# Two decoder layers on one core: which engine copies layer 0's results out of PSUM

## The chip, the cores and the metric

The kernel runs on one core of a Trainium2 chip. The time is the device time of one execution in microseconds (us). A core has five engines with a queue each, which work in parallel and meet through semaphores: PE (TensorE, the matmuls, with its weight loads PEld), DVE (VectorE), ACT (ScalarE), POOL (GpSimd) and SP, which here only issues DMAs. Matmul results land in PSUM, and an engine has to copy them from there to SBUF before a later matmul can read them.

## The reference, cut to what matters

The input x is 4 x 256 x 512 in fp32. Two layers follow each other, each an attention and a linear layer with residuals and layer norms. In layer 0 the attention has 32 heads of 16 channels, in 8 groups of keys and values, with a causal mask:

```python
q = (x @ Wq + bq).reshape(B, S, NUM_HEADS, HEAD_DIM).transpose(0, 2, 1, 3)
k = (x @ Wk + bk)...   # 8 kv heads, each repeated for 4 query heads
scores = jnp.einsum('bhqd,bhkd->bhqk', q, k) / jnp.sqrt(HEAD_DIM)
scores = jnp.where(causal, scores, NEG)
p = jax.nn.softmax(scores, axis=-1)
out = jnp.einsum('bhqk,bhkd->bqhd', p, v).reshape(B, S, D_MODEL) @ Wo + bo
x = _layernorm(x + out)
x = _layernorm(x + x @ W.T + bias)      # W dequantised from q_vals, q_scales
```

Layer 1 does the same with 32 heads of 128 channels, biases by distance, and another linear layer. The change doesn't touch it.

## The kernel before, in words

Layer 0 runs in 64 steps, one for each (b, qt, e, i): four sequences b; two tiles qt of 128 query tokens; and two times four groups e, i of four heads. A step with qt = 0 sees 128 keys, one with qt = 1 sees 256, so that eight steps of 128 keys and eight of 256 take turns. `begin0` (L477) makes a step's scores: four matmuls with 32 rows each (L486) into `sc`, which is four PSUM banks and has one buffer only (`ps_s0`). DVE adds the causal mask while it moves them to SBUF (L489) and takes the negated maximum of each row (L495); ACT makes the exponentials, one instruction for each of four heads with the sum as a second output (L278); DVE inverts the sums (L283) and POOL multiplies by them (L286).

`run` (L327) sets the order. Iteration n calls `before0` for step n, then `begin0` for step n; then `fill` advances the work that fills PE's gaps; then `transpose0` is called for step n-4, and `end0` for step n-6. `transpose0` transposes the probabilities on PE, one PSUM bank with four 128 x 128 blocks for each 128 keys (L301), and has the bank copied to `prT` by `evacuate`: one copy for a step of 128 keys, two for one of 256. After eight steps `end0` has multiplied `prT` with the values (L534) into `o`, which is copied to `oT`, and starts `tail0` for that tile of tokens: output projection py (L442), norm, transpose to `x1T`, linear layer pf (L459), norm, transpose to `x2T` for layer 1. The work that `fill` advances is these tails, the dequantisation and transposition of the linear layer's weight (L206), and `project0` (L372), the q, k and v of the next sequence. The transposes and all these projections share one pool of three PSUM banks, `ps_w`.

Since transposes lag by four steps, the iterations that begin steps of 256 keys copy for four steps of 128 keys and four of 256, and so do those that begin steps of 128. The engine queues in the compiled kernel are not in the order of the code: the framework orders instructions when it compiles, by dependencies and estimated costs of its own, except where the code asks for program order.

`evacuate` (L98) is the one place where the engine of these copies is chosen. It is called for `prT` (L302), for the transposed x, x1 and x2 (L275), for the weight's transposes (L225) and for `oT` (L543). It counts calls, and gives a copy to DVE (L103) or ACT (L105):

```python
if turn[0] % shares[0] == 1 and not last:
    nc.vector.tensor_copy(dst, src)
else:
    nc.scalar.copy(dst, src)
```

In layer 0 `shares[0]` is 3, so that each third copy is DVE's. At L576, after layer 0's loop, it becomes 2, and layer 1 alternates. Layer 1 begins with PE filled by the projections p_k, p_q and p_v (L636), while the last tails of layer 0 end beside it.

Of the kernel before, what the change touches and what calls it, by code (L numbers as in the profile page):

```python
# [61 lines left out]
def block_kernel(  # L62
# [29 lines left out]
    dram = pool(ctx, "dram", 4, space=bass.MemoryType.DRAM)  # L92

    turn = [0]
    shares = [3]
    last = []

    def evacuate(dst, src):  # L98

        if not last:  # L100
            turn[0] += 1
        if turn[0] % shares[0] == 1 and not last:
            nc.vector.tensor_copy(dst, src)  # L103
        else:
            nc.scalar.copy(dst, src)  # L105
# [100 lines left out]
    def feed_forward_weight():  # L206

        for _ in range(G):
            yield True
        nb = D // BLK  # L210
        for oc in range(NC):
            ins = nc.vector.scalar_tensor_tensor(
                wf_n[:, oc, :].rearrange("p (n k) -> p n k", k=BLK),
                qv[:, oc, :].rearrange("p (n k) -> p n k", k=BLK),
                -128.0,
                qs[:, oc, :].unsqueeze(2).to_broadcast([P, nb, BLK]),
                ALU.add,
                ALU.mult,
            )
            tc.keep_in_program_order(ins)  # L220
            yield True
            pw = bank_t(f"pw_{oc}")
            for ic in range(NC):
                nc.tensor.transpose(pw[:, ic, :], wf_n[:, oc, ts(ic, P)], ident)
            evacuate(wfT[:, :, ts(oc, P)], pw)  # L225
        yield True
# [10 lines left out]
    def load_weights1(kv):  # L237
        wq1 = w1.tile([P, NC, G * P], F32, tag="wq1", name=f"wq1_{kv}", bufs=1)
        wo1 = w1.tile([P, G, D], F32, tag="wo1", name=f"wo1_{kv}")
        if kv % 2 == 0:  # L240
            wk1 = w1.tile([P, NC, 2 * P], F32, tag="wk1", name=f"wk1_{kv}", bufs=1)
            nc.sync.dma_start(wk1, w_qkv_v[:, :, NQ + kv * P : NQ + (kv + 2) * P])
            wk_pair[kv // 2] = wk1
        nc.sync.dma_start(wq1, w_qkv_v[:, :, ts(kv, G * P)])
        weights1[kv] = (wq1, wo1)
        if kv == 0:
            load_output_weight(kv)
# [22 lines left out]
    def transposed(dst, src, name):  # L270

        pt = bank_t(f"pt_{name}")
        for c in range(NC):
            nc.tensor.transpose(pt[:, c, :], src[:, ts(c, P)], ident)
        evacuate(dst, pt)  # L275
# [20 lines left out]
    def transposed_probabilities(name, pr, parts):  # L296

        for kt, dst in parts:
            pt = bank_t(f"pt_{name}_{kt}")
            for i in range(G):  # L300
                nc.tensor.transpose(pt[:, i, :], pr[:, i, ts(kt, P)], ident)  # L301
            evacuate(dst, pt.rearrange("p i (j q) -> p i j q", q=32))  # L302
# [43 lines left out]
    def advance(queue):  # L346

        while queue:
            if next(queue[0], None) is not None:
                return  # L350
            queue.popleft()

    def exhaust(queue):
        while queue:
            advance(queue)
# [189 lines left out]

    def before0(step):
        b, qt, e, i = step
        if (qt, e, i) == (0, 0, 0):
            if b == 0:
                for _ in range(3):  # L550
                    advance(ahead)
            else:
                exhaust(ahead)
            if b + 1 < B:
                ahead.append(project0(b + 1))
            if b == 1:
                load_weights1(0)

    def fill():
# [8 lines left out]
        transpose0,  # L568
        end0,
        before0,  # L570
        fill,
        lag=4,
        more=2,
        rest=divide0,
    )
    shares[0] = 2  # L576
    la.close()


# [527 lines left out]
```

## Time and profile before

| what | us |
|---|---|
| median of three runs | 951.85 |
| the three runs | 948.67, 951.85, 1353.63 |
| profiled execution, its own time | 951.23 |
| its span, from first to last instruction | 949.3 |
| PE busy in the span | 906.8 (96%) |
| DVE busy | 623.8 (66%) |
| ACT busy | 333.9 (35%) |
| POOL busy | 444.7 (47%) |

The profile is of one execution. Busy times are of an engine's instructions, a matmul's end is modelled, so that a busy PE is not a PE at its peak. Rows of groups give: line, engine, operation, output and input by the program's names, shapes and count; busy time and mean ns of one; idle time just before them and what ended it. Rows of the timeline give start, length, engine, line and operation, and in brackets the idle time before and what ended it. Layer 0 takes about the first 260 us; its steps of 256 keys begin at 38.5, 98.1, 160.4 and 217.2 us.

### The profile page before, as it was taken

The page shows a single profiled execution, that of the slowest core. Times are in us where ns is not written, and L with a number is a line of the kernel's source. Part 1 is how long each engine was busy: PE and PEld are TensorE (multiplying, and loading weights), DVE is VectorE, ACT ScalarE, POOL GpSimd, SP SyncE. Part 2 cuts the span into 40 slices and gives each one's busy share as a digit, 9 for nine tenths or more (in the row PEclk, how much of TensorE's full clock was granted, in tenths as well). Part 3 has the DMA queues.
Part 4 walks back from the last instruction along what each step waited for, and adds up shares of the span by engine and source line. Part 5 has one row for each costly group of instructions (what it writes and reads, how often), then busy time and mean ns, then how long its engine had stood idle before and what let it go on. Part 6 is the DMA issues. An engine that isn't in the chain of part 4 may idle for free.

```text
span 949.3 us, 11860 instructions
## 1 busy us (share of the span) xinstructions
PE 906.8 (96%) x3849; PEld 554.4 (58%) x3849; DVE 623.8 (66%) x1269; ACT 333.9 (35%) x1216; POOL 444.7 (47%) x462
## 2 busy tenths in 40 slices
PE   7998999898899999999999999999999999999996
PEld 5755555554444445666666566666666666667652
DVE  3986978879434448555676776666666666666566
ACT  2775675677410003323222222122221121214441
POOL 2554553645356124426434533643553534656732
PEclk9999999999999999999999999999999999999998
DMA  9500000000020103543443443353353333432001
GB/s 246 185 1 1 1 2 1 1 1 1 1 89 22 45 1 89 152 111 115 114 130 79 134 132 100 110 140 88 117 139 95 122 89 105 129 89 70 1 34 55
DMA packets 76419, 74.46 MB, mean 78 GB/s; under 512 B 5957, under 2 KB 52678, under 8 KB 76358
## 3 DMA queue, kind: packets, MB, share of 16 engines
q1 hardware_dynamic: 75014, 72.02, 26.4%
q10 hardware_dynamic: 1344, 1.70, 0.6%
q8 instruction: 30, 0.49, 0.2%
q14 instruction: 31, 0.25, 0.1%
HBM read 49.58 MB, written 24.12 MB: 78 GB/s over the span
## 4 chain that ended last, share of the span: by engine, by line
PE 70%; DVE 12%; POOL 9%; ACT 5%; DMA 2%; issue 1%; ACTq 0%; POOLq 0%; SPq 0%; DVEq 0%
PE p_q L636 19%; PE po L885 14%; PE sc L972 7%; PE o L1012 7%; PE p_k L636 5%; PE p_v L636 5%; ACT pr L278 4%; PE py L442 3%; DVE pr L489 3%; PE pf L459 2%; DVE nm L495 2%; PE py L846 2%; POOL x L907 2%; POOL pr L286 2%; DVE prT L103 1%
## 5 line engine op out<-in xcount | busy, mean ns | idle before, releaser
L286 POOL TENSOR_TENSOR pr<-pr,sums 128x512 f32<-128x512 f32 (+1 forms) x128 | 189.5, 1481 | 232.9 <-DVE sums L283 227.4
L278 ACT ACTIVATE pr<-sc,nm 128x128 f32<-128x128 f32 (+1 forms) x256 | 105.0, 419 | 291.1 <-DVE nm L988 277.1
L278 ACT ACTIVATE pr<-pr,nm 128x128 f32<-128x128 f32 (+1 forms) x256 | 113.2, 444 | 39.3 <-DVE sums L283 30.2
L980 DVE SCALAR_TENSOR_TENSOR sc<-table,sc 128x128 f32<-128x128 f32 (+1 forms) x256 | 86.0, 356 | 34.7 <-PE sc L972 32.4
L972 PEld LDWEIGHTS sc<-kT,qT 128*128 128x128 f32 x512 | 82.3, 191 | 35.1 <-issue 29.7
L972 PE MATMUL sc<-kT,qT 128*128 128x256 f32 (+1 forms) x512 | 95.0, 327 | 0.0
L1012 PE MATMUL o<-prT,v 128*128 128x512 f32 x192 | 92.9, 592 | 0.0
L312 DVE STREAM_TRANSPOSE blocks<-pr 128x512 f32<-128x512 f32 x84 | 57.6, 698 | 45.2 <-POOL pr L286 45.1
L650 DVE TENSOR_TENSOR qT<-p_q,qT 128x512 f32<-128x512 f32 x96 | 64.6, 686 | 33.6 <-PE p_q L636 32.8
L988 DVE TENSOR_REDUCE nm<-sc 128x2 f32<-128x512 f32 (+1 forms) x128 | 70.0, 550 | 1.5
L489 DVE TENSOR_TENSOR pr<-sc,causal 128x512 f32<-128x512 f32 (+1 forms) x64 | 60.5, 945 | 10.2 <-PE sc L486 10.0
L301 PE MATMUL pt<-ident,pr 128*128 128x128 f32 x432 | 59.9, 276 | 7.2 <-DVE prT L103 2.1
L495 DVE TENSOR_REDUCE nm<-pr 128x4 f32<-128x512 f32 (+1 forms) x64 | 60.7, 948 | 1.2
L301 PEld LDWEIGHTS pt<-ident,pr 128*128 128x128 f32 x432 | 48.6, 141 | 21.2 <-issue 10.1
L105 ACT COPY o<-o 128x512 f32<-128x512 f32 x29 | 17.0, 587 | 124.9 <-PE o L1012 124.9
L885 PE MATMUL po<-wo,so 128*128 128x256 f32 x224 | 58.0, 381 | 2.1 <-POOL so L616 2.1
L636 PE MATMUL p_q<-x2T,ws_q 128*128 128x512 f32 x128 | 59.8, 592 | 0.0
L636 PE MATMUL p_q<-xt,ws_q 128*128 128x512 f32 x128 | 57.7, 592 | 0.0
L885 PE MATMUL po<-wo,o 128*128 128x256 f32 x224 | 57.7, 380 | 0.0
L636 PE MATMUL p_q<-x2T,wq 128*128 128x512 f32 x128 | 57.6, 592 | 0.0
L105 ACT COPY prT<-pt 128x512 f32<-128x512 f32 x76 | 42.6, 582 | 39.5 <-PE pt L301 39.5
L885 PE MATMUL po<-to,so 128*128 128x256 f32 x224 | 53.3, 381 | 1.0 <-POOL so L619 1.0
(159 smaller groups left out, 1516.8 us busy)
## 6 DMA issues: line engine op xcount, KB each, us to landing
way<-blocks SPq DMA_DIRECT2D x112, 128.0 KB, 2.5
prT<-way SPq DMA_DIRECT2D x28, 512.0 KB, 3.7
wq<-in_L_attn_w_qkv_dram SPq DMA_DIRECT2D x8, 1024.0 KB, 5.1
wo<-in_L_attn_w_o_dram SPq DMA_DIRECT2D x8, 1024.0 KB, 5.4
way<-blocks SPq DMA_DIRECT2D x112, 64.0 KB, 1.8
prT<-way SPq DMA_DIRECT2D x28, 256.0 KB, 2.6
wk<-in_L_attn_w_qkv_dram SPq DMA_DIRECT2D x4, 512.0 KB, 3.8
wv<-in_L_attn_w_qkv_dram SPq DMA_DIRECT2D x2, 1024.0 KB, 6.2
```

The costliest lines, as they stand in the source:

```text
L278: nc.scalar.activation(pr[:, i, 0:w], sc, AF.Exp, bias=nm[:, i : i + 1], accum_out=sums[:, i : i + 1])
L286: nc.gpsimd.tensor_tensor(pr[:, :, 0:w], pr[:, :, 0:w], sums.unsqueeze(2).to_broadcast([P, G, w]), ALU.mult)
L301: nc.tensor.transpose(pt[:, i, :], pr[:, i, ts(kt, P)], ident)
L489: nc.vector.tensor_tensor(pr[:, :, 0:w], sc[:, :, 0:w], causal[:, 2 * P - w :].unsqueeze(1).to_broadcast([P, G, w]), ALU.add,)
L495: nc.vector.tensor_reduce(nm, pr[:, :, 0:w], AX.X, ALU.max, negate=True)
L636: nc.tensor.matmul(bank, fixed, moving, start=(c == 0), stop=(c == 1))
L650: add = lambda dst, a, b: nc.vector.tensor_tensor(dst, a, b, ALU.add)
L885: nc.tensor.matmul(bank[:, ts(n, HALF)], left[:, c, :], right[:, c, :], start=(c == 0), stop=(c == 1),)
L972: nc.tensor.matmul(sc[:, m, 0:w], qT[:, 2 * j + m, b * S + qt * P : b * S + (qt + 1) * P], kT[:, b * S : b * S + w], start=True, stop=True,)
L980: nc.vector.scalar_tensor_tensor(sc[:, m, 0:w], table[:, 2 * P - w :], slopes[kv * G + 2 * j + m], sc[:, m, 0:w], ALU.mult, ALU.add,)
L988: nc.vector.tensor_reduce(nm[:, 2 * j : 2 * j + 2], sc[:, :, 0:w], AX.X, ALU.max, negate=True)
L1012: nc.tensor.matmul(o, v1[:, 2 * b + kt, ts(kv, P)], prT[:, kt].rearrange("p j h q -> p h j q"), start=(kt == 0), stop=(kt == qt),)
```

## The change

The share is now a pattern which the counter walks through, and it depends on the kind of the step that begins in this iteration. With 128 keys (qt = 0) two of three copies go to DVE; with 256 keys (qt = 1) none does. After the last step the pattern of 256 keys stays in force until the loop of layer 0 has ended, and layer 1 has the pattern (0, 1).

```diff
-    shares = [3]
+    shares = [(1, 1, 0)]
...
-        if turn[0] % shares[0] == 1 and not last:
+        if shares[0][turn[0] % len(shares[0])] and not last:
             nc.vector.tensor_copy(dst, src)
         else:
             nc.scalar.copy(dst, src)
...
     def before0(step):
         b, qt, e, i = step
+
+        shares[0] = ((1, 1, 0), (0,))[qt]
         if (qt, e, i) == (0, 0, 0):
...
-    shares[0] = 2
+    shares[0] = (0, 1)
```

## The prediction, made before the changed kernel had run

> **What bounds the kernel now.** I read the page first, for where TensorE (PE) is short of work:
>
> ```profile
> PE   7998999898899999999999999999999999999996
> ...
> DVE  3986978879434448555676776666666666666566
> ACT  2775675677410003323222222122221121214441
> ```
>
> Each digit is a fortieth of the span, 23.7 us. From the twelfth slice (260 us) on PE is full: layer 1 waits for matmuls and nothing else, so a microsecond won or lost in layer 0 arrives at the end whole, and only layer 0 is at stake. Next I cut layer 0 into the stretches in which it begins steps of 256 keys (first, third, fifth and seventh line) and of 128 keys, by the start times of the mask additions of L489. The columns are us, then busy time of PE, weight loads, DVE (VectorE), ACT (ScalarE), POOL, then the granted clock:
>
> ```profile
> 38.50:67.60 29.10, 26.92 (x187) 16.83 (x186) 25.61 (x39) 21.70 (x71) 15.39 (x11) 0.94 0.01 1
> 67.60:98.10 30.50, 28.08 (x188) 16.92 (x187) 20.41 (x44) 18.73 (x79) 13.62 (x13) 1.00 0.00 1
> 98.10:130.20 32.10, 28.85 (x195) 17.71 (x196) 28.97 (x44) 20.87 (x71) 17.42 (x13) 1.00 0.01 2
> 130.20:160.40 30.20, 29.16 (x192) 17.17 (x191) 21.10 (x46) 19.36 (x80) 13.78 (x13) 1.00 0.00 1
> 160.40:192.30 31.90, 29.02 (x195) 17.67 (x195) 29.07 (x44) 21.13 (x72) 17.29 (x13) 1.00 0.00 1
> 192.30:217.20 24.90, 22.44 (x168) 12.35 (x167) 18.53 (x40) 18.51 (x77) 12.49 (x12) 1.00 0.00 1
> 217.20:244.00 26.80, 22.47 (x144) 11.45 (x144) 24.59 (x38) 21.22 (x74) 15.90 (x11) 1.00 0.00 1
> ```
>
> In the 256-key stretches DVE is busy 108.2 of 119.9 us (90%), ACT 84.9 (71%); in the three 128-key ones DVE 60.0 of 85.6 (70%), ACT 56.6 (66%). Yet PE is above 83% everywhere, so this is no plain DVE bound. What PE waits for from 24 to 260 us, with total, times and longest:
>
> ```profile
> PE sc L486 <- DVE pr L489: 8.6, 13, 1.5
> PE py L442 <- ACT oT L105: 3.3, 6, 0.7
> PE pt L301 <- DVE prT L103: 2.1, 2, 1.1
> PE pt L301 <- ACT prT L105: 1.9, 4, 0.7
> ```
>
> All PE waits of that window, with another 1.2 for an oT copied on DVE and small ones, come to 21.6 us: the ceiling of any gain by this change, 2.3%. The largest is the scores' single set of banks, which DVE's mask addition must empty before the next step.
>
> **The change, part by part.** Followed through the code, the counter of `evacuate` reaches 132 in both versions. Before, 44 copies go to DVE: 20 of 59 in iterations that begin a 256-key step, 20 of 60 in 128-key ones, 3 of 10 after the last step, 1 of 3 in layer 1. After, it is 0 of 59, 39 of 60, 0 of 10, 1 of 3. Layer 1 alternates on the same parity as before, so nothing changes there. Prices:
>
> ```profile
> L105 ACT COPY prT<-pt 128x512 f32<-128x512 f32 x64 | 35.9, 579 | 33.8 <-PE pt L301 33.8
> L103 DVE COPY prT<-pt 128x512 f32<-128x512 f32 x32 | 21.7, 678 | 1.3 <-PE pt L301 1.3
> ```
>
> The Trainium skill, "ScalarE: Activation LUTs", section "Rules for kernel authors", puts simple elementwise work (add, mul) on VectorE and not on ScalarE. If a copy counted as such, moving 20 of them to ACT would be a loss; by the rows it is a gain of 0.1 us of engine time each, 2.0 us for 20, given back by the 19 that go the other way. I take the rows: these copies read PSUM in fp32. So no work disappears; it changes place.
>
> *256-key stretches.* DVE loses 20 x 0.678 = 13.6 us, to 94.6 of 119.9 (79%); ACT gains 20 x 0.579 = 11.6, to 96.5 (80%). Averages do not price this; the bursts do, in which PE has little other work. In them a step costs DVE 1.21 + 1.21 + 0.17 = 2.6 us (addition, maximum, reciprocal), and ACT 2.08 (four exponentials in the chain) plus, in the second half of the stretch, two copies, 1.15: 3.2. Before, with a third of two copies on DVE, it was 3.05 against 2.85. So the burst goes from DVE-bound to ACT-bound at much the same rate. Replayed on the timeline, the third stretch of the table above:
>
> ```profile
> 117.07 0.51 ACT L278 ACTIVATE pr<-pr,nm 128x256 f32<-128x256 f32 x1 [2.30 <-DVE sums L283]
> ...
> 119.43 0.66 DVE L103 COPY oT<-o 128x512 f32<-128x512 f32 x1
> ...
> 120.14 3.70 PE L442 MATMUL py<-wop,oT 128*128 128x512 f32 x8 [1.20 <-DVE oT L103]
> ```
>
> Without the DVE copy of prT at 115.18 (0.67 us), the maximum, the exponentials and the next addition come 0.6 earlier. The moved copy fits in ACT's 2.30 us pause. The exponentials end at 118.55, then prT and oT in turn on ACT, 119.7, so py starts at 119.7 in place of 120.14: -0.5. At 48 to 56 us ACT has no such pause (idle 0.3 before each group of exponentials): two moved copies push oT and py from 55.87 to about 56.5, +0.6. At 175 to 182 the 0.6 won on DVE is spent on a third copy in a row on ACT: 0. At 228 to 236: two more copies against a 0.95 pause, +0.2. Together +0.3. Bounds: all waits ended by DVE in these stretches vanish (6.05 by the addition, 2.2 by copies): -8.3; or each of the 20 stands behind a group of exponentials and costs PE the 0.7 of the longest ACT waits: +14. The replay is nearest to the rows and is taken.
>
> *128-key stretches.* 16 of the 19 copies are in the three stretches: DVE +10.8, to 70.9 of 85.6 (83%), ACT -9.3, to 55%. Gains: x1T of tile 0 and oT of tile 1 leave the ACT queue, where PE waited 0.43 (73.9 us) and 0.73 (88.4) for them: -1.2. Loss: five waits for the addition (2.6 us in all) can each have a copy of 0.6 put in front; half of that, +1.5. Bounds -2.6 and +6. Taken +0.3. The cover is the runs of projections (py and pf last 3.7 us each), in which DVE works off what it owes; without it all 10.8 would show.
>
> *The first 128-key stretch*, 24.0 to 38.5, has DVE at 13.04 of 14.5. Three more copies (2.0 us) make 15.1, over the stretch: +0.6 (bounds 0 and 2.0). The one in front of the dequantisation delays PE's pw transposes, already waiting 1.35 there.
>
> *After the last step* the transposes at 244.68 waited 1.10 for a DVE copy that stood behind an addition; on ACT it follows two copies at 243.4: -0.6. At 253.4 two copies ran on both engines at once; on ACT in a row: +0.6. Sum 0. No DMA, buffer or queue of SP or POOL moves.
>
> *The clock.* One stretch ran throttled:
>
> ```profile
> 52.00:56.00 4.00, 2.25 (x23) 0.61 (x19) 3.96 (x7) 3.63 (x13) 2.49 (x3) 1.00 0.00 0
> 56.00:60.00 4.00, 4.00 (x6) 1.71 (x7) 2.12 (x3) 3.63 (x15) 3.44 (x2) 0.58 0.02 4
> ```
>
> After 4 us at 56% busy the clock fell to 0.58, and a py of 3.7 us took 5.4, 1.7 us lost. The Trainium skill, "TensorE: Matmul & The Clock Gate", section "What's actually happening", has the clock fall after an idle window of about 3.4 us. By that rule nothing here is near it (PE's longest wait is 1.55) and the sum gets no term; by the row a thin burst is enough, and the term is -1.7 if the change thickens this burst, +1.7 for another that thins. By my replay this burst gets no denser: 0, and 1.7 to the range.
>
> Sum: 0.3 + 0.3 + 0.6 + 0 + 0 = +1.2. The profiled execution took 951.23 (span 949.3), the median of three is 951.85; 951.85 + 1.2 = **953.0 us**.
>
> **The rivals.** *It cancels* (chance 0.52): 953, own range 948 to 958. *DVE was the bound* (0.22): for it speak its 90% and the 8.6 us; against, that ACT is needed by the same steps and rises to 80%. Most of the 8.3 goes, the first stretch takes some back: -6, 946, down to 940; over 2% needs nearly all 21.6 us of waits to go. *The copies stand behind exponentials on ACT* (0.21), the other clear sign: ACT runs in order, a group blocks 2.08 us, and three banks serve transposes and projections alike. For it speak the 3.3 us for oT and 1.9 for prT; against, that the 39 copies already on ACT there cost PE 0.1 us each. At that 0.1 the move costs 2.0 and is covered; it decides from about 0.4 us per moved copy: 20 x 0.5 = +10, 962, with a tail to 975. *The order itself shifts* (0.05): queues are not in code order (a copy stands between an addition and its maximum at 99.25), so another order may be found, either sign, 3 us.
>
> A measurement of this kernel can tell about 2%, 19 us, from no change. Faster by that is the edge of the second case, 0.03; slower the tail of the third, 0.08; within, 0.89. Range: 944 leaves out the lower part of the second case, 962 the upper half of the third.
>
> **What would show it.** 44 copies on DVE become 40, none in 256-key stretches after 40 us; DVE there near 79%, ACT near 80%; waits of PE for DVE's addition fall there, those for ACT's prT and oT rise by about as much; 24 to 38.5 grows by under a microsecond; from p_k (260.4 us) on the same length as before. The sum fails if PE waits for ACT in the 256-key stretches by far more or less than for DVE before, or if layer 1 changes length.

## The result, and the profile after

The changed kernel took 943.61 us (median of seven runs, 942.18 to 946.05) against 951.85 before; the ratio is 0.9934, with a 95% interval of 0.9917 to 0.9952, so -6.3 us (-7.9 to -4.6) on 950. In a second comparison, further down, it was 0.9927 (0.9910 to 0.9944). The first execution of before, 1353.63, was a disturbed one and is left out of every comparison. The forecast was 953, the range 944 to 962. The median lies 0.4 us below the range: the change is worth 0.7%, within 2%, but it goes the other way, and its -6 is the size of the second rival, 946. Some 2 us of the distance to 953 are the base: the forecast stood on 951.85, and in the later comparisons the medians of before were 949.1 to 949.9.

The rows of the page of the changed kernel, in fortieths of a span of 942.5 us:

```profile
PE   7989899898999999999999999999999999999996
...
DVE  3987978888324457655766676667675766666566
ACT  2785765768410014232222222221221122214441
```

PE is full from the eleventh slice on, as it was from the twelfth. Layer 1's first p_k starts at 253.7 us in place of 260.4, and from there to the end it takes 688.8 us, before 688.9. All of the gain is in layer 0, and all of it arrives.

The same stretches as before, cut at the starts of L489's additions, with the columns us, then busy time of PE, weight loads, DVE, ACT, POOL, and the granted clock:

```profile
39.20:66.70 27.50, 24.87 (x183) 15.76 (x182) 23.30 (x34) 23.68 (x77) 15.81 (x11) 1.00 0.01 1
66.70:95.70 29.00, 28.23 (x193) 17.06 (x191) 23.50 (x50) 16.94 (x74) 13.60 (x13) 1.00 0.00 1
95.70:126.40 30.70, 28.31 (x191) 17.24 (x192) 26.60 (x40) 22.81 (x75) 17.45 (x13) 1.00 0.01 2
126.40:156.20 29.80, 28.80 (x197) 17.51 (x195) 23.66 (x50) 16.19 (x72) 13.17 (x13) 1.00 0.00 1
156.20:187.70 31.50, 28.39 (x191) 17.25 (x192) 26.59 (x39) 23.80 (x79) 17.92 (x13) 1.00 0.01 1
187.70:211.80 24.10, 22.64 (x180) 12.63 (x177) 20.27 (x45) 16.87 (x72) 12.75 (x12) 1.00 0.00 1
211.80:236.00 24.20, 19.90 (x137) 10.56 (x130) 21.35 (x32) 21.62 (x77) 15.93 (x11) 1.00 0.00 1
```

The last line ends where the last addition of layer 0 starts. In the prediction's table the last line ends at 244.0, where that addition ends. Cut at its start, the line of before is:

```profile
217.20:242.70 25.50, 21.74 (x140) 11.03 (x140) 23.29 (x36) 20.48 (x73) 15.90 (x11) 1.00 0.00 1
```

So before had 118.6 us in the 256-key stretches, with DVE at 106.9 (90%) and ACT at 84.2 (71%). Now DVE is at 97.8 of 113.9 us (86%) and ACT at 91.9 (81%); in the 128-key stretches DVE is at 67.4 of 82.9 (81%) and ACT at 50.0 (60%). Every stretch of the table is shorter: those of 256 keys by 4.7 us together, of which 1.7 is the clock (below), and those of 128 keys by 2.7. The stretch ahead of the table is 0.4 longer.

What PE waited for, from 24 to 260 us:

```profile
PE sc L486 <- DVE pr L489: 6.1, 14, 1.0
PE py L442 <- ACT oT L105: 6.0, 7, 1.4
PE pt L301 <- ACT prT L105: 2.4, 3, 1.0
PE o L534 <- ACT prT L105: 1.4, 2, 0.7
```

The wait for the mask addition fell by 2.5 us and the wait for oT rose by 2.7, much as forecast. All waits of PE add up to 19.2 us, before 21.6. That is 2.4 of a gain of 6.7 between the two profiles. The weight loads (PEld) waited for the same addition too, and longer; first before, then after:

```profile
PEld sc L486 <- DVE pr L489: 22.1, 26, 2.5
```

```profile
PEld sc L486 <- DVE pr L489: 18.5, 24, 1.7
```

The rest of the gain is in time that the profile calls busy for PE. These are the sums over layer 0, from 17 us to the first p_k, of before and then of after:

```profile
sum 243.40, PE 221.42 PEld 133.17 DVE 192.52 ACT 162.04 POOL 122.45; mean PE 24.60 PEld 14.80 DVE 21.39 ACT 18.00 POOL 13.61
```

```profile
sum 236.70, PE 217.38 PEld 132.21 DVE 190.33 ACT 163.43 POOL 122.80; mean PE 24.15 PEld 14.69 DVE 21.15 ACT 18.16 POOL 13.64
```

PE did the same matmuls in 4.0 us less of "busy". About 1.7 of it is the clock (below); for the rest the groups of PE tell, the values' product o for one, first before, then after:

```profile
L534 PE MATMUL o<-prT,v 128*32 128x512 f32 x192 | 31.2, 601 | 1.0 <-ACT prT L105 0.9
```

```profile
L534 PE MATMUL o<-prT,v 128*32 128x512 f32 x192 | 29.1, 601 | 1.4 <-ACT prT L105 1.4
```

The mean of one is the same 601 ns, their union is 2.1 us shorter: they lie closer together. The Trainium skill, "Trainium Kernel Development and Optimization", section "Performance Expectations", warns that matmul busy time is a bad measure of how close a kernel is to the roofline, since matmuls are pipelined; in this pair of rows it falls by 2.1 us for 192 matmuls of an unchanged mean.

### The profile page after: what moved, and what is told of

Same layout as the page of the kernel before. It is cut to its first block, busy times and chain, and to the rows that moved or that the text cites. A ratio compares the mean times of both kernels' runs of the same rounds, so it can differ in the third digit from the quotient of the medians.

```text
span 942.5 us, 11859 instructions
## 1 busy us (share of the span) xinstructions
PE 902.2 (96%) x3849; PEld 552.9 (59%) x3849; DVE 621.4 (66%) x1265; ACT 335.7 (36%) x1220; POOL 445.0 (47%) x462
## 4 chain that ended last, share of the span: by engine, by line
PE 73%; DVE 10%; POOL 9%; ACT 4%; DMA 2%; issue 1%; ACTq 0%; SPq 0%; POOLq 0%; DVEq 0%
PE p_q L638 19%; PE po L887 14%; PE sc L974 7%; PE o L1014 7%; PE p_k L638 5%; PE p_v L638 5%; PE py L442 3%; ACT pr L278 3%; PE pf L459 3%; DVE pr L489 2%; DVE nm L495 2%; PE py L848 2%; POOL x L909 2%; PE pt L301 2%; POOL pr L286 2%; PE sc L486 1%
## 5 line engine op out<-in xcount | busy, mean ns | idle before, releaser
L489 DVE TENSOR_TENSOR pr<-sc,causal 128x512 f32<-128x512 f32 (+1 forms) x64 | 60.6, 947 | 7.8 <-PE sc L486 7.1
L301 PEld LDWEIGHTS pt<-ident,pr 128*128 128x128 f32 x432 | 48.7, 141 | 19.2 <-issue 8.0
L105 ACT COPY prT<-pt 128x512 f32<-128x512 f32 x82 | 44.7, 586 | 27.4 <-PE pt L301 27.3
```

What stands on the lines that cost most here:

```text
L489: nc.vector.tensor_tensor(pr[:, :, 0:w], sc[:, :, 0:w], causal[:, 2 * P - w :].unsqueeze(1).to_broadcast([P, G, w]), ALU.add,)
```

## The experiments

All ran with timing against the kernel before on the same chip. The differences are ratios times 950 us, with their intervals. The clock is the mean over a kernel's runs of the granted clock; before had 0.9950 to 0.9955. A clock lower by 0.001 is 0.1%, about 1 us here; half_b, below, shows a fall that comes at least in part of the kernel itself, so such a difference is not always chance.

| kernel | 256-key steps, DVE | 128-key steps, DVE | us against before | clock |
|---|---|---|---|---|
| the change | none | 2 of 3 | -6.3 (-7.9 to -4.6) | 0.9957 |
| after_again | none | 2 of 3 | -6.9 (-8.6 to -5.3) | 0.9960 |
| only256 | none | 1 of 3 | -4.2 (-5.2 to -3.0) | 0.9957 |
| only128 | 1 of 3 | 2 of 3 | -0.7 (-2.1 to +0.8) | 0.9942 |
| third2 | another third | another third | -1.6 (-2.9 to -0.4) | 0.9949 |
| third0 | another third | another third | -1.5 (-3.2 to +0.1) | 0.9949 |
| allact | none | none | +7.9 (+5.7 to +10.0) | 0.9907 |
| full128 | none | all | -0.5 (-1.9 to +1.0) | 0.9943 |
| half_a | none in the first four | 1 of 3 | -2.6 (-3.8 to -1.2) | 0.9955 |
| half_b | none in the last four | 1 of 3 | +1.4 (+0.1 to +2.8) | 0.9931 |
| dve_load | none, and spare additions | 2 of 3 | +8.4 (+5.9 to +10.8) | 0.9913 |
| dve_load2 | none, and 23 reductions | 2 of 3 | +0.8 (-0.7 to +2.1) | 0.9943 |
| act_load | 1 of 3, and 23 ACT copies | 1 of 3 | +2.6 (+1.4 to +3.7) | 0.9945 |
| dve_a | none, and 8 reductions | 2 of 3 | -1.0 (-2.6 to +0.4) | 0.9936 |
| dve_b | none, and 15 reductions | 2 of 3 | -4.5 (-5.8 to -3.2) | 0.9966 |
| ot_dve | none but oT | 2 of 3 and oT | -7.1 (-9.5 to -4.7) | 0.9966 |
| best | none but oT | 1 of 3 at first, then 2 of 3; oT | -9.8 (-11.8 to -7.9) | 0.9968 |

**The two halves of the change, and all on ACT.** The patterns are edited where the change set them:

```diff
# only256
-    shares = [(1, 1, 0)]
+    shares = [(0, 1, 0)]
-        shares[0] = ((1, 1, 0), (0,))[qt]
+        shares[0] = ((0, 1, 0), (0,))[qt]
# only128
-        shares[0] = ((1, 1, 0), (0,))[qt]
+        shares[0] = ((1, 1, 0), (0, 1, 0))[qt]
# allact
-    shares = [(1, 1, 0)]
+    shares = [(0,)]
-        shares[0] = ((1, 1, 0), (0,))[qt]
+        shares[0] = ((0,), (0,))[qt]
```

> Half of the change: steps of 256 keys all on ACT, steps of 128 keys as before (one of three on DVE). Theory A (DVE set the pace in the 256-key stretches, relief there is the gain): all of it or more, -6 to -8 us against before. Theory B (the recorded one: DVE's relief and ACT's load cancel there): 0 to +1. Theory C (scatter: any other choice of which third of the copies goes to DVE moves the time by several us): no rule, between -6 and +6.

> The other half: steps of 128 keys two of three on DVE, steps of 256 keys as before. Theory A: +1 to +3 us against before, DVE gets 19 more copies and nothing in return. Theory B: +1. If the gain of the whole change lies in the 128-key stretches, because ACT is relieved there, -3 to -5.

> All copies of layer 0 on ACT, in steps of 128 keys too: DVE is relieved in both stretches, ACT takes 43 copies more. Theory A: in the 256-key stretches as good as the change; in the 128-key ones ACT rises from 66% to about 80%, DVE falls to 58%, so -5 to -9 us against before if only DVE counts, and worse than the change if the two of three on DVE matter there. Theory B: 0 to +5.

only256 won 4.2 us, two thirds of the whole; by the prediction's account it had to be 0 to +1. only128 is not to be told from before, at a lower mean clock (0.9942 against 0.9953, 1.0 us of the span); the rest of the change beside only256 is 2.1 us. allact lost 7.9, so it was not DVE alone that counted: in the 128-key steps a third of the copies on DVE is worth 12 us. There the exponentials and all copies stand in one queue, and where PE is short of work the clock is low too. Four stretches of 4 us in the profile of allact, with the columns as above:

```profile
72.00:76.00 4.00, 3.21 (x15) 2.37 (x14) 1.46 (x3) 2.92 (x11) 1.36 (x2) 0.50 0.00 0
76.00:80.00 4.00, 4.00 (x12) 2.40 (x11) 0.00 (x0) 2.71 (x10) 0.60 (x1) 0.66 0.01 4
212.00:216.00 4.00, 2.06 (x14) 1.09 (x15) 2.04 (x5) 3.39 (x16) 2.08 (x2) 0.91 0.00 0
216.00:220.00 4.00, 4.00 (x7) 1.53 (x6) 0.00 (x0) 0.28 (x2) 0.00 (x0) 0.67 0.00 0
```

At 0.50 to 0.91 the clock costs about 5 us in these 16; the stretches themselves are 34.5 and 31.7 us long, before 30.5 and 24.9.

**All on DVE in 128-key steps.**

```diff
# full128
-    shares = [(1, 1, 0)]
+    shares = [(1,)]
-        shares[0] = ((1, 1, 0), (0,))[qt]
+        shares[0] = ((1,), (0,))[qt]
```

> Steps of 256 keys all on ACT, steps of 128 keys all on DVE. All-ACT in the 128-key steps cost 12 us against one in three on DVE, and two of three won another 1 to 2. If DVE at two of three is near its limit (83% in the table): +2 to +6 against the changed kernel. If ACT's relief still counts: -1 to -3 against the changed kernel, -7 to -9 against before.

The 256-key steps stay on ACT; DVE's share of the copies in 128-key steps is none, one, two or three of three in allact, only256, the change and full128: +7.9, -4.2, -6.3, -0.5. Two of three is near the best of these, and both ends cost. The first 128-key stretch of full128 took 23.7 us, before 21.7, in the change 22.1: there DVE has the weight's dequantisation as well. The four 128-key stretches of full128 are 6.1 us longer than those of the change.

**Scatter: another third.** Two kernels give DVE one copy in three everywhere, as before, but others.

```diff
# third2
-    shares = [(1, 1, 0)]
+    shares = [(0, 0, 1)]
-        shares[0] = ((1, 1, 0), (0,))[qt]
+        shares[0] = ((0, 0, 1), (0, 0, 1))[qt]
# third0: the same with (1, 0, 0)
```

> One copy of three on DVE in all steps, as before, but the next third of them (43 DVE copies in layer 0 in place of 43, other ones). Theories A and B: within 1.5 us of before. Theory C: it moves by 4 us or more, either way, and the result of the change is no proof of a mechanism.

> A second other choice of one copy in three for DVE in all steps (43 in layer 0, as before; five oT and two x1T among them). Scatter of the choice alone: within 2 us of before if the load counts, 4 us or more either way if the choice does.

Both came out about 1.5 us below before, third2 clear of zero and third0 just not. So the choice of copies, at the same load, can move the time by that much; a gain of 6 is more than this scatter, the 0.7 of only128 is not.

**What a load costs.** The first attempt added unused additions on DVE; `extra` is a flag that is on in 256-key steps and at the end:

```diff
# dve_load, on the change
+            if extra and turn[0] % 3 == 1:
+                nc.vector.tensor_tensor(spare, fb_b, fb_b, ALU.add)
```

> The changed kernel, with an idle DVE addition of 128x512 in SBUF (0.69 us) traced at each place in the 256-key steps and at the end where the copy was DVE's before: 23 of them, which nobody waits for. DVE has its old load back, ACT keeps the copies. Theory A (DVE's load was the cost): the 256-key gain of about 4 us is lost, so -1 to -3 against before. If only the place of the copies mattered, not the load: -5 to -7, as the changed kernel. If ACT's load were the gain's limit: no change either.

It went to +8.4 and says less than it seems. The timeline shows all 23 additions between 36.5 and 89 us, and some of them 1.2 to 2.3 us long beside POOL: they depend on nothing, and the ordering at compile time pulled them forward. The next two tie the spare work to its place by its input:

```diff
# dve_load2, on the change; out is a slice of spare in the shape that is needed
+        if extra and turn[0] % 3 == 1:
...
+            nc.vector.tensor_reduce(out, dst, AX.X, ALU.max)
# act_load, on the kernel before, in the same places
+        if extra and turn[0] % 3 == 1:
...
+            nc.scalar.copy(out, dst)
```

> The changed kernel, with a reduction on DVE of each tile that a moved copy has just written (128x512, about 0.68 us, result unused), at the 23 places in 256-key steps and at the end where the copy was DVE's before. Unlike the spare additions of the earlier run it can't run ahead of its place. DVE has its old load back there, ACT keeps the copies. If DVE's load was what the 256-key half won, the time goes back by 4 us or more: -2 to +4 against before. If DVE has slack there, it stays within 1.5 us of the changed kernel: -5 to -7.

> The kernel before, with a second copy on ACT of each tile that DVE copied in a 256-key step or at the end (SBUF to SBUF, about 0.6 us, unused). ACT has the changed kernel's load there, DVE keeps its own. If the prediction's ACT bound is real (ACT 80% busy costs about what DVE's relief gains): +4 or more against before. If ACT has slack in those stretches: within 1.5 us of before.

Against the changed kernel (ratio 0.993 in the mean of its two comparisons) dve_load2 lost 7.4 us: 23 reductions of 0.66 us cost 0.32 each. act_load lost 2.6 against before: 23 copies of 0.62 us cost 0.11 each. 7.4 less 2.6 is 4.8, about the 4.2 that only256 won. In its wait list the price of dve_load2 is seen at once (the added code moves these lines down by 9):

```profile
PE sc L495 <- DVE pr L498: 12.5, 12, 2.9
PE py L451 <- ACT oT L106: 3.1, 6, 0.7
```

The wait for the mask addition doubled from the 6.1 of the changed kernel. In act_load it stayed about as it was before (8.3, before 8.6), and what rose is the wait for oT:

```profile
PE sc L495 <- DVE pr L498: 8.3, 13, 1.2
PE py L451 <- ACT oT L106: 4.5, 6, 1.1
```

Each spare instruction also waits for the copy that it reads (1.2 and 1.1 us in two waits on DVE, 6.0 us in six on ACT), so both prices are upper ones. And the price of dve_load2 is not spread evenly: 3.8 of the 7.3 us between its profile and that of the change lie in the last stretch, where one DVE instruction took 2.11 us in place of 0.55. The next runs show the same thing.

**Where DVE's load bites.** First by halves of the 256-key relief:

```diff
# half_a (half_b: (1, 1)), on the change
-    shares = [(1, 1, 0)]
+    shares = [(0, 1, 0)]
-        shares[0] = ((1, 1, 0), (0,))[qt]
+        shares[0] = (0,) if (qt, e) == (1, 0) else (0, 1, 0)
```

> Only the first four steps of each 256-key stretch are all on ACT; everything else has one of three on DVE, as before. In these iterations each transposed step brings one copy. Theory A1 (the gain lies where PE looked full, outside the bursts that the prediction replayed): about half or more of the 4.2 us that the whole 256-key half won, -2 to -4. Theory B1 (the gain comes from the bursts in the second half, and the replay was wrong): within 1 us of before.

> Only the last four steps of each 256-key stretch (and the end of layer 0) are all on ACT; the rest as before. These iterations hold the bursts, with two copies for each transposed step. Theory A1: within 1.5 us of before. Theory B1: -3 to -5.

Then by halves of the load:

```diff
# dve_a (dve_b: e == 1), on dve_load2
-        extra[:] = [True] * qt
+        extra[:] = [True] * (qt == 1 and e == 0)
```

> The changed kernel with the unused DVE reductions of 0.68 us in the first four steps of each 256-key stretch only (8 of the 23). If DVE's load costs the same everywhere (7 us for 23): +2.4 against the changed kernel. If PE's projections cover DVE there, as the prediction held: below +1.

> The same reductions in the last four steps of each 256-key stretch and after the last step (15 of the 23). Same price everywhere: +4.6 against the changed kernel. If all of DVE's price lies here, in the bursts: +6 to +8. If the bursts are ACT's, as the prediction's replay had it: below +2.

The first four steps won 2.6 us by themselves. half_b lost 1.4, so the two don't add up to the 4.2 of only256. In the profile the loss of half_b has one place: its last stretch took 29.2 us, that of only256 24.2.

```profile
228.18 1.89 POOL L286 TENSOR_TENSOR pr<-pr,sums 128x1024 f32<-128x1024 f32 x1
228.25 2.11 DVE L268 TENSOR_SCALAR x<-y,mv_b,rs_b 128x512 f32<-128x512 f32 x1 [0.58 <-POOL rs_b L264]
...
230.27 1.21 DVE L489 TENSOR_TENSOR pr<-sc,causal 128x1024 f32<-128x1024 f32 x1
...
231.54 1.24 PE L486 MATMUL sc<-kT,qT 32*128 32x256 f32 x8 [3.26 <-DVE pr L489]
```

L268 is the last instruction of a norm. Here it took 2.11 us, beside a multiplication on POOL. In only256 it began ahead of that multiplication:

```profile
227.51 0.52 DVE L268 TENSOR_SCALAR x<-y,mv_b,rs_b 128x512 f32<-128x512 f32 x1
```

In half_b the mask addition behind it came late, PE waited 3.26 us for that, and from 230 to 238 us the clock was 0.57 and 0.58. So the low mean clock of half_b, 0.9931 against 0.9955 and worth 2.3 us, belongs at least in part to this place. Elsewhere the last four steps won as they do in the change: in each of the first three 256-key stretches of half_b the time from py to the end is 0.5 us shorter than before, the clock apart.

Against after_again, dve_a lost 5.9 us for 8 reductions, at a clock 0.0024 lower, and dve_b 2.5 for 15, at one 0.0006 higher. That is not a price by halves: 4.7 of the 6.6 us between the profiles of dve_a and after_again lie in the last stretch, where the same instruction (L277 there) again took 2.11 us, PE waited 2.96 and the clock fell to 0.54. In dve_b's profile this doesn't happen. Without that stretch a reduction cost 0.3 us in dve_a (1.8 for six), and in dve_b 0.2 (2.7 for all 15). A place of such a price, from the timeline of dve_a:

```profile
48.09 0.69 DVE L113 TENSOR_REDUCE spare<-prT 128x16 f32<-128x512 f32 x1 [1.10 <-ACT prT L106]
...
48.70 1.21 DVE L504 TENSOR_REDUCE nm<-pr 128x4 f32<-128x1024 f32 x1
...
51.16 0.71 PE L495 MATMUL sc<-kT,qT 32*128 32x256 f32 x8 [0.91 <-DVE pr L498]
```

The maximum, ready since 47.0, starts at 48.70, and PE waits 0.91 us for the addition behind it. It shows as well that a wait inside DVE's queue is part of this price, so 0.3 is an upper value too.

**Versions beyond the change.** PE waited 6.0 us for oT on ACT in the changed kernel, and its first 128-key stretch had lost 0.4.

```diff
# ot_dve, on the change, in end0
-            evacuate(oT.rearrange("p i q -> p (i q)"), o)
+            turn[0] += 1
+            nc.vector.tensor_copy(oT.rearrange("p i q -> p (i q)"), o)
# best, on ot_dve
-    shares = [(1, 1, 0)]
+    shares = [(0, 1, 0)]
-        shares[0] = ((1, 1, 0), (0,))[qt]
+        shares[0] = ((1, 1, 0) if b else (0, 1, 0), (0,))[qt]
```

> The changed kernel once more, as the base for the three others of this call: -5 to -7 us against before.

> The changed kernel, with all eight copies of oT on DVE. In the changed kernel PE waited 6.0 us for seven copies of oT that stood behind exponentials on ACT. If the wait is ACT's order, DVE at 79% takes them sooner: -2 to -4 us against the changed kernel, -8 to -10 against before. If the copy waits as long behind additions and maxima of 1.2 us on DVE: 0 to +2 against the changed kernel.

> The changed kernel with oT always copied by DVE, and with one copy in three on DVE, as before, in the first 128-key stretch, where the changed kernel lost 0.4 us. -7 to -8.5 against before, 1 to 2 below the changed kernel; if neither matters, the same as the changed kernel.

best took 939.7 us, 9.8 below before; its four runs (939.45 to 940.93) lie below all of after_again's on the same chip (941.90 to 944.38). ot_dve alone is not to be told from the change. PE still waits 5.9 us for oT, now on DVE, so the reason that I gave for ot_dve fell. What changed is the order. The first oT and py in best:

```profile
52.16 0.68 DVE L544 COPY oT<-o 128x512 f32<-128x512 f32 x1
...
52.94 3.70 PE L442 MATMUL py<-wop,oT 128*128 128x512 f32 x8
```

Counted from the first addition of its stretch py starts at 16.1 us here, in the change at 17.9, after a burst in which PE had little to do. Here it fills the burst; that stretch took 25.6 us, in the change 27.5 with a full clock and, in the profile of after_again, 29.2 with a low one. In ot_dve's profile it took 26.0.

## Why the prediction failed, point by point

**The step that failed** is the price of the 256-key stretches, "Averages do not price this; the bursts do", with its +0.3. The half of the change that it prices measured -4.2 (only256). The replay itself was good. From the start of the addition to the start of py the four bursts changed by +0.6, -0.5, 0 and -0.1; forecast were +0.6, -0.5, 0 and +0.2. The third stretch's burst in the changed kernel:

```profile
110.59 1.57 ACT L105 COPY prT<-pt 128x512 f32<-128x512 f32 x3 [0.64 <-PE pt L301]
...
115.73 0.57 ACT L105 COPY prT<-pt 128x512 f32<-128x512 f32 x1
116.19 0.58 ACT L105 COPY oT<-o 128x512 f32<-128x512 f32 x1
...
116.83 1.13 PE L442 MATMUL py<-wop,oT 128*128 128x512 f32 x2 [1.22 <-ACT oT L105]
```

The moved copy sits in ACT's pause, prT and oT follow in turn, and py starts 5.65 us after the addition at 111.18 (before 6.10). But the bursts are some 23 of 119 us. Ahead of them the four stretches won 0, 0.5, 0 and 0.7 us, and from py to the end about 0.5 each, the clock apart. Those were the parts in which PE looked full. The replay left them out of the sum, as if projections covered DVE's copies there. They did not: half_a moves only copies of the first four steps and won 2.6 us, and in its profile the parts ahead of the bursts are 0.5, 0.2, 0.6 and 0.7 us shorter than before, while the four bursts changed by 0.1 at most.

**The size of both loads.** In these stretches DVE's relief is worth up to 7.4 us, half of it in one place, and ACT's load costs up to 2.6. The 2.6 stood in the prediction: "At that 0.1 the move costs 2.0", in the third rival, from the 39 copies already there. The likeliest case took the ACT-bound replay in its stead. The second rival, "DVE was the bound", had the sign and the size. Of its mechanism the runs bear out that DVE's load was the cost, but not that most of the 8.3 us of visible waits would go: PE's waits for the addition fell by 2.5. A third of the change's gain, moreover, came with its 128-key half, where DVE took copies on. The loads themselves were set too high: DVE's busy time in the 256-key stretches fell by 9.1 us and not by 13.6, ACT's rose by 7.7 and not by 11.6. 18 copies left there and not 20, and rows of one engine overlap: the copy of 0.68 us at 99.25 has the next instruction behind it at 99.85. The 79% forecast for DVE became 86, since the stretches got shorter as well.

**The ceiling of 21.6 us** was none in kind: of 6.7 us only 2.4 came out of PE's waits.

**The 128-key stretches**, forecast +0.3: of the two gains named the 0.43 for x1T is there, of the 0.73 for oT only 0.2, since PE waits 0.53 for it on DVE. The loss of 1.5 by copies in front of additions is not there: PE's waits for the addition in these three stretches fell from 2.6 us to 1.4. All three are shorter, by 1.5, 0.4 and 0.8. The half is worth between -0.7 (only128) and -2.1 (beside only256). That DVE does have a limit there full128 shows: a third more costs 5.8.

**The first stretch**, forecast +0.6: 22.1 us in place of 21.7, in the change as in only128; right in sign and nearly in size. **The end of layer 0**, forecast 0: 17.6 in place of 17.7. **Layer 1**: unchanged, right.

**The clock**, forecast 0 with 1.7 either way. The same 8 us in the profile of after:

```profile
52.00:56.00 4.00, 3.25 (x24) 0.77 (x22) 3.58 (x5) 4.00 (x17) 3.66 (x2) 1.00 0.00 0
56.00:60.00 4.00, 2.88 (x7) 1.44 (x8) 2.87 (x5) 3.77 (x16) 2.45 (x2) 1.00 0.02 4
```

The clock stayed full, and the stretch is 1.6 us shorter for it. That is chance and not the change: after_again, the same kernel, had 0.83 and 0.74 there. The mean clock of the change's runs is 0.9957 and 0.9960, that of before 0.9950 to 0.9955; in the comparison that has both it is 0.0006, worth 0.6 us. In only256, 12 runs at 0.995 took 947.15 us and 7 at 0.997 took 945.02 in the mean. The Trainium skill, "TensorE: Matmul & The Clock Gate", section "What's actually happening", says that the window runs free, so that the point of transition varies; that fits. Its idle window of about 3.4 us does not, if that means 3.4 us without matmuls: before, where the clock fell to 0.58, PE's longest wait from 52 to 56 us was 1.02. The 3.26 us of half_b come nearer. The row that I weighed it against was the better guide.

**What stays open.** The prices per instruction contain waits in order, which no run separates. half_b, dve_a and dve_load2 have one profile each, so whether L268 takes 2.11 us in all their runs is not known. How much of the rest is load and how much is the new order of PE's queue isn't told apart either: third2 and third0 put the choice alone at 1.5 us, and ot_dve shows that one moved copy can reorder a whole burst. Why best won more than ot_dve is open as well: their profiles differ by 0.8 us in layer 0, and their intervals overlap.

## What to carry to other kernels

When copies can go to either of two engines, price them stretch by stretch by the engine that has less room there, and let neither take all. An engine at 90%, as DVE here, can cost time also where no wait of the bottleneck is drawn: replaying the visible stalls gave their sizes to 0.3 us and still missed the gain. Measure a load's price by adding unused work that is tied to its place by its input; in dve_load, work without one was moved elsewhere by the ordering. And look for instructions that took longer than others of their kind before dividing the price by a count.

## What the runs showed of the hardware that was not expected

Copying 128x512 from PSUM stayed shorter on ACT (585 ns) than on DVE (679), and still a copy taken off DVE was worth more than it cost on ACT, 0.32 us against 0.11 by the spare loads, both upper values. The granted clock fell to 0.58 after 4 us with PE 2.25 us busy (before, 52 to 56 us) and to 0.50 after 4 us with 2.81 (allact, 68 to 72 us), yet stayed at 1.00 in the change through 4 us with 2.88; and for one and the same kernel it was 1.00 in one profile and 0.74 in another (after and after_again, 56 to 60 us). The same DVE instruction on 128x512 in fp32, from SBUF to SBUF, took 0.52 us in only256 and 2.11 in half_b, dve_a and dve_load2, where it ran beside a multiplication of 1.89 us on POOL; PE's wait list puts the 3.26 us behind it in half_b down to DVE.
